# Scattering expert results into token order with an adding transfer, and moving the last expert blocks into the last attention

## The chip, the cores and the metric

The kernel runs on one core of a Trainium2 chip. The metric is the device time of one execution in microseconds (us). Five engines run beside one another, each through its own list of instructions in order: TensorE (PE) multiplies matrices, VectorE (DVE) and ScalarE (ACT) work element by element, GpSimd (POOL) does so too and issues indirect transfers, and SyncE (SP) issues plain transfers. They wait for one another through semaphores. Transfers run on 16 DMA engines that all queues share.

## The reference

There are 8 images of 256 channels and 1024 positions (32 x 32), in float32. Three parts follow one another for each image:

```python
# layer 0: attention with 8 heads of 64, the softmax over the queries
qkv = xt @ w_qkv + b_qkv                       # (8, 1024, 1536)
attn = softmax(einsum('bihd,bjhd->bijh', q, k) * SCALE, axis=1)
x = einsum('bijh,bjhd->bihd', attn, v) @ w_out + b_out + xt
# layer 1, attention over the 1024 tokens of an image
n = ln(t);  t = t + softmax((n @ W.T) @ n.T) @ n
# layer 1, experts: each token goes to the best two of eight
n = ln(t)
combine = weights of the two best of softmax(n @ router_w.T), normalised
out = n
for e in range(8):
    y = gelu(n @ w1[e] + b1[e]) @ w2[e] + b2[e]
    out = out + combine[:, e] * y
t = t + out
```

All sizes of the expert part are 256. The output goes back to channels by positions.

## The kernel before, in words

The main loop at the end of the function goes through the images b = 0 to 7. For each it calls `layer0` (the 8-head attention, in which PE alternates score products and value products), `attend` (the second attention) and `normed` (the norm and the router's logits). While `attend` runs, a function `fill(place)` is called at named places, to put other work into PE's gaps: for images 0 to 6 that is `Begin.at`, which computes the next image's values and its first queries and keys.

Images 0 to 6 form one group of 7168 tokens. For each of them `dispatch` works out, on DVE, a row for every token and each of its two experts, in a DRAM table `rows` that has one stretch of 7168 rows for each expert. Sixteen indirect transfers on POOL (L1081), one for each 128 tokens and choice, write the normed tokens there; they are sent one by one during the next image's `layer0`. The table is filled with zeros at the start (`prepare`, 7 transfers of 8 MB, L295). The token's own sum so far (t2 plus its norm) is kept in DRAM as `sums`, one 1 MB tensor for each image.

When image 7 is in its `layer0`, `plan` counts the tokens of each expert and divides them into 63 blocks of 256 rows, with an address of rows and of weights for each. `experts` then runs the 63 blocks between `layer0` and `attend` of image 7. A block passes through these steps, in different turns of one loop:

- `fetch`: SP loads 256 rows as four transfers (L1252), into one of four buffers; `turned` transposes them on DVE (L1258).
- `hidden`: PE multiplies by the first weight matrix (`ph`, L1269) and ACT applies gelu (`hb`, L1279).
- `collect`: PE multiplies by the second matrix (`pe`, L1295), DVE adds the bias and writes `yb` (L1305, two buffers). POOL issues the gather of the weights for the block four ahead (L1235, which moves nothing if the weights are the same as those in place) and then stores `yb` as rows of a DRAM tensor `y` (L1312).

In the same loop DVE takes one step of `places` for a block, which works out, for each token, where its two results lie in `y`.

`Results` brings the results home. It runs beside `attend` and `dense` of image 7, and a table `PLACES` says at which of their steps how many units are gathered, added and stored. A unit is 128 tokens: two indirect gathers from `y` on POOL (L1391), two multiply-adds on DVE with the gates as factors (L1413), into a tile loaded from `sums`. When an image is whole, `store` transposes each half on DVE (L1449) and sends it out with four transfers of SP.

Image 7 itself has its experts in `dense`: all eight experts on all 1024 tokens, 16 steps of 512 tokens, each with a first product (L1518), a gelu (L1527), a second product (L1542) and four multiply-adds of DVE (L1551).

In `attend` the scores of two blocks of 128 tokens are a `Pair`; `turn` transposes a block of the softmax with DVE and with 16 moves of 32 partitions (L844), half by ACT and half by transfers of SP; `turn_now` does so on PE; `mix` multiplies it by the tokens (`py`, L861). Every engine's instructions run in the order in which the program lists them; `issue_after` and `add_manual_dep` put an instruction behind another.

Of the kernel before, what the change touches and what calls it, by code (L numbers as in the profile page):

```python
# [10 lines left out]
F32 = mybir.dt.float32  # L11
# [8 lines left out]
def kernel(  # L20
# [40 lines left out]
    NXB = NWB + 1  # L61
    SQ = 32
# [3 lines left out]
    WHOLE = 1.5 * 2**23  # L66
# [174 lines left out]

    class Norm:
# [42 lines left out]
    def prepare():  # L285

        zero = wbs[0][:, : 2 * D]
        with tc.issue_after(evicted[0, 0, 1].ins):
            nc.vector.memset(zero, 0.0)

        def fill(group):

            per = E * group.cap // (2 * P)
            return [
                nc.sync.dma_start(  # L295
                    group.rows.rearrange("(p c r) d -> p c (r d)", p=P, r=2)[:, c : c + 32],
                    zero.unsqueeze(1).to_broadcast([P, 32, 2 * D]),
                )
                for c in range(0, per, 32)
            ]  # L300

        first = fill(groups[0])[0]
        with tc.issue_after(first.ins):
            pack()

# [79 lines left out]
    class Begin:  # L385
# [36 lines left out]
        def at(self, place):  # L422

            if place == "norm 1":
                self.project(True)
            elif place == "norm 2":
                with tc.issue_after(evicted["mixed"].ins):
                    self.project(True)
            self.values(1)
# [248 lines left out]
    def attend(b, t1, fill, tick=nothing):  # L678
# [51 lines left out]
        class Pair:  # L730
# [19 lines left out]
            def middle(self, behind=None):  # L750
                far = self.ex[1][:, HALF:]
                with tc.issue_after(behind.ins) if behind else nullcontext():
                    self.product(self.x, s2_, t2_, False)
                self.second = nc.scalar.copy(self.ex[0][:, HALF:], self.x)
# [73 lines left out]
        def turn(i, ex, behind=None):  # L828
# [11 lines left out]
            for a in range(NQ):  # L840
                for k in range(NQ):
                    move = nc.sync.dma_start if (a + k) % 2 else nc.scalar.copy
# [37 lines left out]
        pairs = [Pair(0).middle(), Pair(1).middle()]  # L880
# [6 lines left out]
        pairs[2].middle(evicted["mixed"])  # L887
# [5 lines left out]
        mix(*third)  # L893
        pairs[3].middle()
# [85 lines left out]
    class Group:  # L980


        def __init__(self, n, items):
# [3 lines left out]
            self.rows = dram.tile([E * self.cap, D], F32, name=f"rows_{n}")  # L987
            self.views = dram_disjoint_views(self.rows, 2 * NT * len(items))
            self.y = dram.tile([self.nb * BR, D], F32, name=f"y_{n}")
            self.sums = [dram.tile([P, NT, D], F32, name=f"sums_{b}") for b in items]  # L990
            self.counts = None
            self.kept = {}
# [3 lines left out]
    def normed(b, t2, fill, tick=nothing, norm=None):  # L996

        if norm is None:
            n2 = one.tile([P, NT, D], F32, tag="n", name=f"n2_{b}")
            tick("normed", layer_norm(t2, n2, 1e-5, f"f{b}"))  # L1000
        else:
            n2 = norm.dst
# [3 lines left out]
        tick("turned", to_channels(n2, nT, f"n2_{b}"))  # L1006

        nc.gpsimd.tensor_add(t2, t2, n2)  # L1008
# [4 lines left out]
    def dispatch(b, n2, l, group):  # L1013
# [44 lines left out]
        kept = []  # L1058
        ats = []
        for k in range(2):  # L1060
# [3 lines left out]
            row = keep.tile([P, NT], F32, tag=f"row{k}", name=f"row{k}_{b}")  # L1064
            nc.vector.tensor_reduce(row, sel, AX.X, ALU.add)
            nc.vector.tensor_mul(sel, hot, e_iota.unsqueeze(1).to_broadcast([P, NT, E]))
            exp = keep.tile([P, NT], F32, tag=f"exp{k}", name=f"exp{k}_{b}")
# [3 lines left out]
            kept.append((row, exp))  # L1071
# [3 lines left out]
        group.kept[b] = gate, kept  # L1075

        for k in range(2):
            for i in range(NT):
                behind = yield
                view = group.views[2 * (NT * group.items.index(b) + i) + k]  # L1080
# [9 lines left out]
    def plan(group):  # L1090
# [6 lines left out]
        def tmp(tag, shape, dtype=F32):  # L1097
# [16 lines left out]
        first = keep.tile([P, E], F32, tag="first", name=f"first_{n}", bufs=2)  # L1114
# [5 lines left out]
        turns = keep.tile([P, 1], F32, tag="turns", name=f"turns_{n}", bufs=2)  # L1120
# [17 lines left out]
        nc.vector.tensor_add(block, block, after)  # L1138
        base = tmp("p_base", [E])
        nc.vector.tensor_scalar_mul(base, first, -float(BR))  # L1140
        nc.vector.tensor_scalar(
            first[:, E // 2 :], first[:, E // 2 :], left, None, ALU.subtract
        )
        group.first = first, turns
# [9 lines left out]
        nc.vector.tensor_scalar_min(e_of, e_of, float(E - 1))  # L1154
# [12 lines left out]
        nc.vector.tensor_scalar_min(lo, lo, float(cap - BR))  # L1167
        nc.vector.scalar_tensor_tensor(lo, e_of, float(cap), lo, ALU.mult, ALU.add)
        row_at = keep.tile([P, NBMAX], I32, tag="row_at", name=f"row_at_{n}", bufs=2)
# [14 lines left out]

    def places(group):

        first, turns = group.first
        for b in group.items:
            gate, kept = group.kept[b]
            ats = []  # L1190
            for k, (row, exp) in enumerate(kept):
                hot = small.tile([P, NT, E], F32, tag="d_sel", name=f"p_hot_{b}_{k}", bufs=1)
                nc.vector.tensor_tensor(
                    hot,
                    exp.unsqueeze(2).to_broadcast([P, NT, E]),
                    e_iota.unsqueeze(1).to_broadcast([P, NT, E]),
                    ALU.is_equal,
                )
                nc.vector.tensor_mul(
                    hot, hot, first.unsqueeze(1).to_broadcast([P, NT, E])  # L1200
                )
                to = small.tile([P, NT], F32, tag="d_to", name=f"p_to_{b}_{k}", bufs=2)
                nc.vector.tensor_reduce(to, hot, AX.X, ALU.add)
                nc.vector.scalar_tensor_tensor(to, to, float(BR), row, ALU.mult, ALU.add)
                yield
                pos = small.tile([P, 2, NT], F32, tag="d_pos", name=f"p_pos_{b}_{k}", bufs=2)
                nc.vector.tensor_scalar(
                    pos[:, 0], to, 0.5 - BR / 2, 1.0 / BR, ALU.add, ALU.mult
                )
                nc.vector.tensor_scalar_add(pos[:, 0], pos[:, 0], WHOLE)  # L1210
                nc.vector.tensor_scalar(pos[:, 1], exp, E / 2 - 0.5, None, ALU.is_gt)
                nc.vector.scalar_tensor_tensor(
                    pos[:, 0], pos[:, 0], -WHOLE, pos[:, 1], ALU.add, ALU.add
                )
                nc.vector.tensor_scalar(
                    pos[:, 0], pos[:, 0], turns, float(BR), ALU.min, ALU.mult
                )
                nc.vector.tensor_add(to, to, pos[:, 0])
                at = keep.tile([P, NT], I32, tag=f"yat{k}", name=f"yat{k}_{b}")
                nc.vector.tensor_copy(at, to)  # L1220
                ats.append(at)
                if k > 0:
                    group.kept[b] = gate, ats
                yield

    def experts(group, behind):
# [17 lines left out]
        def fetch(b):  # L1244
            xr = rowp.tile([P, RUN, DQ], F32, tag="xr", name=f"xr_{n}_{b}")
            with tc.issue_after((loads[-1] if loads else evicted["relayed"]).ins):
                at = nc.sync.value_load(
                    row_at[0:1, b : b + 1], min_val=0, max_val=E * group.cap - BR
                )
            mine = group.rows[bass.ds(at, BR), :].rearrange("(s t) (k d) -> k t s d", s=RUN, k=NQ)  # L1250
            for k in range(NQ):
                loads.append(nc.sync.dma_start(xr[ts(k, SQ)], mine[k]))  # L1252
            return xr
# [10 lines left out]
        def hidden(b, xb):  # L1264
# [11 lines left out]
            hT = two.tile([P, NFC, BR], F32, tag=f"qk{b % 2}", name=f"hb_{n}_{b}")  # L1276
# [11 lines left out]
        def collect(b, hT, last, squares):  # L1288
# [3 lines left out]
            with tc.issue_after(last.ins):  # L1292
                for r in range(R):
                    for fc in range(NFC):
                        nc.tensor.matmul(  # L1295
# [8 lines left out]
            with tc.issue_after(squares.ins):  # L1304
                added = nc.vector.tensor_add(  # L1305
# [3 lines left out]
                )  # L1309
            if b + NXB < group.nb:  # L1310
# [341 lines left out]
```

## Time and profile before

| what | value |
|---|---|
| median of 3 runs | 2332.85 us (2331.51 to 2340.35) |
| the profiled execution's own time | 2328.95 us |
| its span, first to last instruction | 2327.1 us |
| PE, DVE, ACT, POOL busy | 97%, 67%, 50%, 18% of the span |
| last `layer0` ends, expert blocks begin | about 1870 us |
| first and last yb add of the expert blocks (L1305) | 1876.1 and 2097.8 us |
| first scores product of the last attention (L708) | 2099.65 us |
| first product of the dense stage (L1518) | 2195.22 us |

A line of the profile names the place in the kernel (L1305), the engine, the operation, the tiles written and read (`yb<-pe,wb`), and, in brackets, how long the engine was idle before it and what ended that. POOL's "busy" for a transfer is the time to issue it; the transfer lands later, which shows only in the wait of an instruction that needs it. "issue" is idle time for which the profile shows no releaser. The median of the runs stands 3.9 us above the profiled execution.

### The profile page before, as it was taken

Reading aid. Unit: us, or ns where it says so; the run is one execution under the profiler, and the core shown is the slowest. Engines: PE = TensorE matmul, PEld = TensorE weight load, DVE = VectorE, ACT = ScalarE, POOL = GpSimd, SP = SyncE. Lnnn points to the kernel's source line nnn. Section 1 sums busy time; section 2 is a strip of 40 time slices with the busy share of each in tenths; the row PEclk is TensorE's granted clock in tenths of the full one; section 3 lists DMA queues with packets and bytes.
Section 4 is the critical chain, followed back from the end, with each engine's and each line's share of the span. In section 5 each row is a group of like instructions: output and inputs, shape, how many; then the busy total and the mean of one; then the engine's idle time right before and its main releaser. Section 6 shows DMA issues by size and latency. Waiting matters only on the chain.

```text
span 2327.1 us, 37989 instructions
## 1 busy us (share of the span) xinstructions
PE 2261.6 (97%) x13059; PEld 1216.1 (52%) x13059; DVE 1554.5 (67%) x4029; ACT 1163.0 (50%) x2138; POOL 410.7 (18%) x392
## 2 busy tenths in 40 slices
PE   9999999999999999999999999999999999998798
PEld 3345533563456335643564355435553488884565
DVE  5775687567855786578657775777568766436655
ACT  3664466456635663656365646465646622225211
POOL 0000012000200020003000200020002135545563
PEclk9999999999999999999999999999999999999899
DMA  8995201020103010201020101100111157765574
GB/s 294 385 386 154 68 17 39 9 56 13 44 2 62 8 49 1 46 19 53 3 46 19 49 8 29 36 26 13 23 42 42 49 145 192 192 199 145 154 210 113
DMA packets 278759, 200.10 MB, mean 86 GB/s; under 512 B 189576, under 2 KB 232232, under 8 KB 276776
## 3 DMA queue, kind: packets, MB, share of 16 engines
q1 hardware_dynamic: 252472, 139.14, 21.2%
q0 software_dynamic: 25008, 58.01, 7.8%
q8 instruction: 104, 1.70, 0.3%
q10 hardware_dynamic: 1088, 0.52, 0.1%
q14 instruction: 87, 0.71, 0.1%
HBM read 108.88 MB, written 110.90 MB: 94 GB/s over the span
## 4 chain that ended last, share of the span: by engine, by line
PE 80%; ACT 5%; DVE 4%; issue 4%; DMA 3%; POOL 3%; SPq 1%; another core or an unknown queue 0%; DVEq 0%; ACTq 0%; POOLq 0%
PE po L569 19%; PE psc L492 19%; PE py L861 7%; PE pqk L371 7%; PE pr L671 5%; PE pv L408 4%; PE ps L761 4%; PE ph L1269 3%; PE pe L1295 3%; PE px L708 2%; POOL yk L1391 2%; PE pqk L349 2%; PE ps1z L761 2%; DMA y<-yb 1%; ACT aT L844 1%
## 5 line engine op out<-in xcount | busy, mean ns | idle before, releaser
L533 ACT ACTIVATE ex<-psc,nmax 128x1024 f32<-128x1024 f32 x512 | 570.0, 1114 | 299.8 <-DVE scrap L516 217.4
L492 PE MATMUL psc<-qk,qk 64*64 64x512 f32 x4096 | 575.8, 593 | 3.8 <-ACT ex L533 3.5
L569 PE MATMUL po<-ex,vs 64*64 64x512 f32 x4096 | 570.6, 591 | 3.6 <-DVE vs L549 2.6
L516 DVE TENSOR_SCALAR_CACHE_REDUCE scrap<-psc,nmax 128x512 f32<-128x512 f32 x512 | 384.2, 750 | 160.3 <-PE psc L492 133.6
L507 DVE TENSOR_REDUCE nmax<-psc 128x1 f32<-128x512 f32 x512 | 350.1, 684 | 9.3 <-PE psc L492 9.3
L492 PEld LDWEIGHTS psc<-qk,qk 64*64 64x64 f32 x4096 | 180.4, 132 | 279.2 <-ACT ex L533 132.6
L569 PEld LDWEIGHTS po<-ex,vs 64*64 64x64 f32 x4096 | 176.5, 132 | 275.6 <-DVE vs L549 82.1
L1081 POOL DMA_INDIRECT rows<-n,d_at x112 | 109.0, 973 | 661.1 <-DVE nmax L507 660.8
L1008 POOL TENSOR_TENSOR t<-t,n 128x2048 f32<-128x2048 f32 x8 | 36.3, 4535 | 875.5 <-DVE n L263 875.5
L371 PE MATMUL pqk<-xT,wqkv 128*128 128x512 f32 x384 | 171.2, 599 | 0.0
L861 PE MATMUL py<-n,spare 128*128 128x256 f32 x512 | 122.0, 394 | 11.3 <-DMA out_dram<-oT 3.8
L336 ACT ACTIVATE qk<-pqk,b_qks 128x512 f32<-128x512 f32 x124 | 85.6, 690 | 86.7 <-PE pqk L371 77.6
L1391 POOL DMA_INDIRECT yk<-y,yat x112 | 111.3, 994 | 76.4 <-issue 28.4
L371 PEld LDWEIGHTS pqk<-xT,wqkv 128*128 128x128 f32 x384 | 71.0, 190 | 99.9 <-issue 77.0
L408 PE MATMUL pv<-wqkv,xT 128*128 128x512 f32 x256 | 121.5, 599 | 1.5 <-DVE v L416 1.0
L861 PEld LDWEIGHTS py<-n,spare 128*128 128x128 f32 x512 | 100.7, 198 | 38.1 <-issue 23.9
L671 PE MATMUL pr<-wo,res 128*128 128x256 f32 x512 | 111.9, 379 | 0.7 <-ACT res L588 0.7
L844 ACT COPY spare<-home 32x256 f32<-32x256 f32 x256 | 103.0, 402 | 10.0 <-DVE home L833 6.7
L671 PEld LDWEIGHTS pr<-wo,res 128*128 128x128 f32 x512 | 97.2, 190 | 17.7 <-ACT res L588 4.7
L1279 ACT ACTIVATE hb<-ph,wb 128x256 f32<-128x256 f32 x96 | 40.1, 470 | 126.9 <-issue 89.4
L533 ACT ACTIVATION_READ_ACCUMULATOR ex<-psc,nmax 128x1 f32 x512 | 99.1, 194 | 0.0
L870 DVE SCALAR_TENSOR_TENSOR t<-py,rs,t 128x256 f32<-128x256 f32 x64 | 30.5, 476 | 98.0 <-PE py L861 85.3
(256 smaller groups left out, 2939.7 us busy)
## 6 DMA issues: line engine op xcount, KB each, us to landing
rows<-wb SPq DMA_DIRECT2D x7, 8192.0 KB
xr<-rows SPq DMA_DIRECT2D x252, 64.0 KB
y<-yb POOLq DMA_DIRECT2D x63, 256.0 KB
xs<-in_x_dram SPq DMA_DIRECT2D x64, 128.0 KB
spare<-home SPq DMA_DIRECT2D x256, 32.0 KB
out_dram<-oT SPq DMA_DIRECT2D x60, 128.0 KB
xT<-in_x_dram SPq DMA_DIRECT2D x7, 1024.0 KB
sums<-t SPq DMA_DIRECT2D x7, 1024.0 KB
```

The costliest lines, as they stand in the source:

```text
L371: mm = nc.tensor.matmul(pq[:, ts(n, 512)], wqkv[:, cc, t, ts(g, P)], xT[:, cc, ts(n, 512)], start=(cc == 0), stop=(cc == NCC - 1),)
L408: nc.tensor.matmul(pv, self.xT[:, cc, ts(i, P)], wqkv[:, cc, 2, :], start=(cc == 0), stop=(cc == NCC - 1),)
L492: mm = nc.tensor.matmul(pss[at, h][ts(c, DK), ts(n, 512)], k[r, j * P + c * DK : j * P + (c + 1) * DK], q[r, ts(n, 512)], start=True, stop ...
L507: firsts[at, h] = nc.vector.tensor_reduce(nmax, pss[at, h][:, ts(0, 512)], AX.X, ALU.max, negate=True)
L516: seconds[h] = nc.vector.tensor_scalar(scrap, pss[at, h][:, ts(1, 512)], -1.0, nmaxes[at, h], ALU.mult, ALU.min, accum_out=nmax,)
L533: nc.scalar.activation(ex, pss.pop((at, h)), AF.Exp, bias=nmaxes.pop((at, h)), scale=1.0, accum_out=sums[at][:, h : h + 1],)
L569: mm = nc.tensor.matmul(po[n][ts(h, DK), :], vss[at][keys, h, :], exps[at, h][keys, ts(n, 512)], start=(j == 0 and turn == 0), stop=(j == ...
L671: nc.tensor.matmul(pr[:, :C], res[:, g, ts(i, P)], wo[:, g, :], start=(g == 0), stop=(g == NPAIR - 1))
L761: return nc.tensor.matmul(to, stationary[:, ts(self.k, P)], moving, start=start, stop=True, skip_group_check=not start,)
L844: move(to[ts(k, SQ), a], since[ts(a, SQ), k])
L861: evicted["mixed"] = nc.tensor.matmul(py[:, :D], aT[m], n1[:, m, :], start=(m == 0), stop=(m == NT - 1))
L1391: ins = nc.gpsimd.indirect_dma_start(out=self.slot(at)[:, k, :], out_offset=None, in_=self.group.y[:, :], in_offset=bass.IndirectOffsetOnAxis(
```

## The change

It has three parts.

1. *Rows carry gate and destination.* A row of `rows` has 258 numbers instead of 256: the token, its gate, and a number that gives its place in `sums`. POOL writes the two columns (a copy and an iota) before each group of eight row scatters. `sums` becomes one tensor of 14336 rows in token order, twice: the first half begins as each image's own sum, the second half as zeros (`clear`, one 7 MB transfer of SP ahead of image 1). In `experts`, a fifth load a block brings gate and place (`where`); DVE multiplies `yb` by the gate and works out the place; and two indirect transfers on POOL with an addition in the transfer (128 rows of 1 KB each) add `yb` to `sums`. Rows that no token fills have a place out of bounds and are skipped. `places`, the tensor `y` and its plain store are gone.
2. *`Results`* now loads both halves of an image's sums, 1 MB each, with plain transfers of POOL, adds them with DVE in halves of an image, one at each step of `dense`, and stores them a step later. It begins behind the norm, so nothing of it is left in the last attention.
3. *The last four blocks* (`LATE`) finish inside image 7's attention: their second products at the places "between", "between 2" and "norm 2", and the first products of the last two at "last weights". For this `Pair.middle` is split in two, in all images, one value block of `Begin.at` moves from "last products" to "between", and block 6's `turn` uses two transfers fewer and two ACT copies more. The dense stage's second and third weights are loaded behind the norm instead of ahead of it.

```diff
+    DW = D + 2
 class Group:
-            self.rows = dram.tile([E * self.cap, D], F32, name=f"rows_{n}")
+            self.rows = dram.tile([E * self.cap + BR, DW], F32, name=f"rows_{n}")
-            self.y = dram.tile([self.nb * BR, D], F32, name=f"y_{n}")
-            self.sums = [dram.tile([P, NT, D], F32, name=f"sums_{b}") for b in items]
+            self.sums = dram.tile([2 * self.cap, D], F32, name=f"sums_{n}")
+            self.ways = dram_disjoint_views(self.sums, R * self.nb)
+    def clear(group):
+        pieces = group.sums[group.cap :].rearrange("(p c r) d -> p c (r d)", p=P, r=2)
+        nc.sync.dma_start(
+            pieces,
+            wbs[0][:, : 2 * D].unsqueeze(1).to_broadcast([P, group.cap // (2 * P), 2 * D]),
+        )
 def dispatch:
+                if i == 0:
+                    nc.gpsimd.tensor_copy(n2[:, :, D], gate[:, k, :])
+                    nc.gpsimd.iota(
+                        n2[:, :, D + 1],
+                        [[-1, NT]],
+                        base=2 * group.cap - (k * len(group.items) + which) * S,
+                        channel_multiplier=-NT,
...
 def experts, fetch:
+            where = small.tile([P, R, 2], F32, tag="where", name=f"where_{n}_{b}", bufs=8)
+            loads.append(
+                nc.sync.dma_start(
+                    where, group.rows[bass.ds(at, BR), D:].rearrange("(r p) c -> p r c", r=R)
+                )
+            )
 def experts, collect:
             yb = two.tile([P, R, D], F32, tag="yb", name=f"yb_{n}_{b}")
...
+                where = wheres.pop(b)
+                nc.vector.tensor_mul(yb, yb, where[:, :, 0:1].to_broadcast([P, R, D]))
+                to = small.tile([P, R], I32, tag="to", name=f"to_{n}_{b}", bufs=4)
+                nc.vector.tensor_scalar(
+                    to, where[:, :, 1], -1.0, float(2 * group.cap), ALU.mult, ALU.add
+                )
             if b + NXB < group.nb:
                 weights(b + NXB)
-            nc.gpsimd.dma_start(group.y[ts(b, BR), :].rearrange("(r p) d -> p r d", r=R), yb)
-            if b >= NXB:
-                with tc.issue_after(added.ins):
-                    next(placed, None)
+            for r in range(R):
+                nc.gpsimd.indirect_dma_start(
+                    out=group.ways[R * b + r][:, :],
+                    out_offset=bass.IndirectOffsetOnAxis(ap=to[:, r : r + 1], axis=0),
+                    in_=yb[:, r, :],
+                    in_offset=None,
+                    bounds_check=2 * group.cap - 1,
+                    oob_is_err=False,
+                    compute_op=ALU.add,
+                )
+            return mm
 experts, the loop:
-            if b - 3 in rows:
+            if b - 3 in rows and b - 3 < group.nb - LATE // 2:
-            if b - 4 in hiddens:
+            if b - 4 in hiddens and b - 4 < group.nb - LATE:
 Results:
+            nc.gpsimd.dma_start(self.totals[n], self.group.part(0, n))
+            nc.gpsimd.dma_start(self.seconds[n], self.group.part(1, n))
+            n, h = self.todo.pop(0)
+            some = self.totals[n][:, ts(h, NB), :]
+            with tc.issue_after(behind.ins):
+                nc.vector.tensor_add(some, some, self.seconds[n][:, ts(h, NB), :])
 turn:
-                    move = nc.sync.dma_start if (a + k) % 2 else nc.scalar.copy
+                    away = (a + k) % 2 and (i < 6 or a > 0)
+                    move = nc.sync.dma_start if away else nc.scalar.copy
 the main loop, image 7:
-        experts(groups[0], evicted["divided"])
-        others = Results(groups[0])
-        others.begin()
+        product, result = experts(groups[0], evicted["divided"])
...
+            if place == "between":
+                result(end - 4)
+            elif place == "between 2":
+                result(end - 3)
+            elif place == "last weights":
+                product(end - 2)
+                product(end - 1)
+            elif place == "norm 2":
+                with tc.issue_after(evicted["mixed"].ins):
+                    result(end - 2)
+                    result(end - 1)
```

## The prediction

> **What bounds the kernel now.** I read the page's chain first. It is PE for 80% of the span, and through the first seven images PE is never idle, so nothing that merely frees another engine gains there. The change works on the end, from the expert blocks (about 1870 us) on, so I asked for busy time by stretch: the last image's attention, the same stretch of image 6 (which has no expert results to add), and the expert blocks. The columns are stretch, length, busy time of PE, PEld, DVE, ACT, POOL with instruction counts, granted clock, DMA share, GB/s.
>
> ```profile
> 2099.60:2183.90 84.30, 70.49 (x216) 43.61 (x216) 53.42 (x121) 40.62 (x89) 49.76 (x50) 0.90 0.64 170
> 1634.20:1702.10 67.90, 65.17 (x225) 40.36 (x224) 35.76 (x85) 40.41 (x89) 0.00 (x0) 1.00 0.24 39
> 1878.00:2084.00 206.00, 200.78 (x921) 173.46 (x919) 101.88 (x268) 48.62 (x116) 103.96 (x116) 1.00 0.68 187
> ```
>
> The last attention takes 16.4 us longer than image 6's, with 17.7 us more DVE work: the result adds and output transposes. The expert blocks are PE-bound (97%), but not by much. In the timeline there (start, duration, instruction, idle time before it with its releaser) I followed one yb buffer round:
>
> ```profile
> 1968.42 0.69 DVE L1305 TENSOR_TENSOR yb<-pe,wb 128x512 f32<-128x512 f32 x1 [0.89 <-PE pe L1295]
> 1969.86 1.03 POOL L1235 DMA_INDIRECT wb<-wpack,w_at  x1 [1.66 <-issue]
> 1970.88 0.77 POOL L1312 DMA_DIRECT2D y<-yb  x1
> 1976.22 0.69 DVE L1305 TENSOR_TENSOR yb<-pe,wb 128x512 f32<-128x512 f32 x1 [1.78 <-DMA y<-yb]
> ```
>
> The add fills yb at 1968.42; POOL starts the next weight gather 1.44 us later, then the store; the buffer is free for the next-but-one block when the store has landed, 4.57 us after its issue ended. One turn is 7.80 us. There are two yb buffers, so a turn over 6.90 us (two PE blocks of 3.45) eats slack. The yb tile's own table (us, times) shows that it often does:
>
> ```profile
>   DVE yb L1305: 45.1, 20
> ```
>
> PE keeps its pace only because these waits are occasional. From the first yb add (1876.1) to that of block 58 (2084.82) the mean is 208.7/58 = 3.60 us a block. Last, POOL when its indirect transfers follow one another:
>
> ```profile
> 2208.44 0.95 POOL L1391 DMA_INDIRECT yk<-y,yat  x1 [0.30 <-issue]
> 2209.70 0.99 POOL L1391 DMA_INDIRECT yk<-y,yat  x1 [0.30 <-issue]
> 2210.99 0.95 POOL L1391 DMA_INDIRECT yk<-y,yat  x1 [0.30 <-issue]
> 2212.25 0.95 POOL L1391 DMA_INDIRECT yk<-y,yat  x1 [0.30 <-issue]
> ```
>
> Each starts about 1.26 us after the one before: 0.95 busy and 0.30 of issue. The direct store above followed its gather with no such gap.
>
> **What the Trainium skill says.** "DMA: Bandwidth & Descriptors", Anatomy of one DMA (SWDGE path): most of the fixed cost of a POOL transfer is waiting for the write's receipt, and HBM is the slowest target. The trace agrees: stores land 3.66 to 6.3 us after their issue ends. The same page, Rules for kernel authors: an accumulating DMA reads its destination and writes it later. No accumulating DMA is in this trace. "Collectives: The Full Stack", The bandwidth ceiling: an add in the DMA engine costs a second source read and about halves the rate; not shown here either. "Perfetto Trace Analysis", GPSIMD Engine Instruction: POOL durations are to be taken from start-to-start spacing, which is why I use 1.26 and not 0.95.
>
> **The change, part by part.** *Expert loop.* Out go the small DVE operations that worked out row addresses (0.16 to 0.23 us each, some 11 for two blocks, on a DVE busy 49%): no gain. The one store of a block becomes two indirect scatters with addition; DVE gets a second pass over yb (taken as the add's 0.69, waiting for the add) and one small operation (0.17); SP gets a fifth load a block (8-byte pieces; one issue more at a median of 0.32 us, on a queue that loads up to four blocks ahead, so hidden). In the built program POOL's order is weights, scatter, scatter for each block, and the add of block b waits for both scatters of block b-2. So the turn is: 1.44 to the weight gather, 1.33 to the first scatter (1.03 and 0.30; yb is ready by then, at about 1.44 + 0.3), 1.26 to the second, 0.97 for it (the mean of the row scatters in the page), then L, the landing: 5.00 + L. While DVE waits for it, the transposes of later rows and the adds are queued behind, and PE's next product waits for the accumulator that the add would free. The pace is then half a turn.
>
> L is not in this trace. Lower end: 3.66, the last stores, with little other traffic (issued 2093.40 + 0.72, buffer written at 2097.78). Upper end: 6.26, a store during a weight load (2038.71 + 0.76 to 2045.73). The second scatter has half the bytes but is read and written and has the first just ahead of it; I take 4.8, a little above the loaded 4.57. A gain on L below 3.66 isn't excluded for half the bytes, nor a cost above 6.26 for the addition; both are rivals below.
>
> The turn is 9.8, the pace 4.9. Block 58 is the last whose result is taken in the loop: 1876.1 + 58 x 4.9 = 2160.3, and with 1.5 us for its second pass the attention's first copy (nT) starts at 2161.8. Before, it started at 2098.38, after all 63 blocks. The change is +63.4 us here. That already credits the loop with the products that move out of it (four second products and two first ones, 6 x 1.73 = 10.4 us).
>
> *Last attention.* Image 6 took 67.90. Take out its two value blocks (2 x 1.72), put in two first and two second expert products (4 x 1.73): 71.4, say 72, against 84.3: -12.3. Two more second products fall in the norm, where PE idled 3.48 us. There DVE loses 3.8 us of adds and transposes and gains 2.8 us of expert results: -1.
>
> *Dense stage.* 112 gathers and 112 DVE adds (479 ns) become 14 loads of 1 MB and 14 half-image adds (some 1.25 us each, taken from the 128x1024 transposes). PE lost 3.7 us in 2260 to 2300 behind the gathers: -4. The first load waits for the last scatters, which stand behind the 4.5 us POOL add: about 4.5 + 4 x 1.26 + 4.8 + 7 for 2 MB = 21 us after the norm, some 4 us past its first use, of which PE's other work covers half: +2. Sum -2.
>
> *Hidden parts.* The gate and destination columns and their iotas are on POOL, idle in image 6's attention and nearly so elsewhere. The 7 MB clear goes once on SP, 19 us of DMA at 390 GB/s, beside image 1's PE-bound layer; SP's first zero fill issued in 0.4 us and the next took 21.5, so it is hidden unless a queue entry behind it has to wait for room: then up to 19 us. The reordering of value blocks in the other attentions shifts PE work; image 6 idles 2.7 us, so 0 with at most a few us either way for all seven.
>
> *Sum.* 63.4 - 12.3 - 1 - 2 = +48.1. The profiled execution took 2328.95 (span 2327.1), so 2377 of that kind; the median of the runs is 3.9 above it: 2332.85 + 48.1 = 2381.
>
> **The rivals.** With the tail worth -15.3, the turn decides: the change breaks even when 58 paces = 2098.38 - 1877.6 + 15.3 = 236.1, a pace of 4.07, L = 3.14.
> *B, POOL's issue is the bound.* Three indirect starts a block are 1.33 + 1.26 + 1.26 = 3.85, already over PE's 3.45. If scatters land within 2.7 us it sets the pace: 223.3 - 236.1 = -13, 2320. For it: half the bytes; against: 3.66 for an almost undisturbed store.
> *C, the turn stays hidden and the change is faster.* If the 0.30 gaps overlap and the landing is short, the pace stays at 3.60: 208.8 - 236.1 = -27, 2306 (at 3.45, 2297). Its place is the yb wait; it decides from a turn of 7.2 us down. For it: the tail gain is clear in the profile. Against: the turn is 7.8 today with one transfer.
> *D, the addition is slow.* If a scatter with addition takes L = 8, the pace is 6.5: 377 - 236.1 = +141, 2474. For it: the second read; against: the DMA engines are 68% busy and a block's scatters double only 23% of that (POOL's queue took 35.0% of 16 engines for 25.02 MB in 224 us: 50 ns a KB, so 256 KB over 16 engines is 0.8 of 3.45 us).
> *E, the clear or the reordered attentions stall the front,* the turn as forecast: up to +19, 2400.
>
> **How the numbers follow.** Forecast (L 3.66 to 6.26, so 2348 to 2423; its own range) 0.52, B 0.13, C 0.15, D 0.15, E 0.05. A measurement here can tell about 0.5% (11.7 us) from no change. Faster: C and over half of B, 0.23. Same (2321 to 2345): the rest of B and the forecast's lower edge, 0.09. Slower 0.68. The range reaches from the middle of C, 2304, to the start of D, 2440, leaving out 0.08 and 0.12.
>
> **What would show it.** Right: DVE's yb add idle for most of each block behind the scatters' landing; yb adds of one buffer 9 to 11 us apart; PE about 70% busy in the expert stage; attention 70 to 75 us. Wrong: PE still 95% busy there (C), POOL busy with 0.3 gaps and no DVE wait (B), or turns above 12 us (D).

## The result: 87 us slower, and the profile after

| | before | after |
|---|---|---|
| median (range) | 2332.18 us (2328.99 to 2340.35, 4 runs) | 2419.43 us (2418.46 to 2421.18, 4 runs) |
| span of the profiled execution | 2327.1 us | 2417.9 us |

The ratio is 1.0369, with an interval of 1.0342 to 1.0397. Cut the two profiled executions at the same three events (the first yb add; px, the last attention's first product; and the end of its last product, py), and the 90.8 us between the spans have a place:

| stretch | before | after | difference | forecast |
|---|---|---|---|---|
| start to the first yb add | 1876.1 | 1903.2 | +27.1 | 0 |
| first yb add to px | 223.6 | 308.7 | +85.1 | +63.4 |
| last attention, px to the end of py | 84.2 | 69.4 | -14.8 | -12.3 |
| norm and dense stage, to the end | 143.2 | 136.6 | -6.6 | -3 |

Busy time by stretch of the changed kernel, with the columns of the prediction's table (length; PE, PEld, DVE, ACT, POOL; clock, DMA share, GB/s): the last attention and the expert loop.

```profile
2211.90:2281.30 69.40, 68.75 (x249) 45.03 (x250) 39.36 (x94) 44.38 (x97) 10.85 (x8) 1.00 0.33 58
1903.00:2209.00 306.00, 230.76 (x942) 185.19 (x943) 119.11 (x234) 48.92 (x117) 250.41 (x173) 0.95 0.77 123
```

The attention is full of PE work. In the loop PE has sunk to 75% and POOL has risen to 250.41 busy. POOL issued 173 transfers there, and the timeline shows 0.30 us ahead of each: 250.4 + 173 x 0.30 = 302 of 306 us. POOL's queue is full. One block's turn, in the timeline of the changed kernel (DVE and POOL lines):

```profile
1992.15 0.69 DVE L1324 TENSOR_TENSOR yb<-pe,wb 128x512 f32<-128x512 f32 x1 [3.51 <-DMA sums<-yb,to]
...
1995.31 1.07 POOL L1246 DMA_INDIRECT wb<-wpack,w_at  x1 [0.30 <-ACT hb L1298]
1996.68 1.58 POOL L1338 DMA_INDIRECT sums<-yb,to  x1 [0.30 <-issue]
...
1998.57 1.96 POOL L1338 DMA_INDIRECT sums<-yb,to  x1 [0.31 <-issue]
...
2000.83 1.07 POOL L1246 DMA_INDIRECT wb<-wpack,w_at  x1 [0.30 <-issue]
...
2003.35 0.69 DVE L1324 TENSOR_TENSOR yb<-pe,wb_x 128x512 f32<-128x512 f32 x1 [3.64 <-DMA sums<-yb,to]
```

The block added at 1992.15 has its scatters issued only from 1996.68 on, because POOL is still at the block before and then at the next gather. From there: 1.58, 0.31 and 1.96 us of issue, and the buffer is free at 2003.35, only 2.82 us after the second issue ended. The page has the two kinds of scatter side by side, that with addition and the plain one of the rows, both of 128 rows of about 1 KB:

```profile
L1338 POOL DMA_INDIRECT sums<-yb,to x126 | 206.9, 1642 | 78.9 <-DVE yb L1330 41.3
L1132 POOL DMA_INDIRECT rows<-n,d_at x112 | 109.1, 974 | 515.5 <-DVE nmax L527 476.8
```

One with addition takes 1.64 us of POOL, a plain one 0.97 (means). So a block asks POOL for 1.07 + 1.64 + 1.64 + 3 x 0.30 = 5.25 us, and the first 59 yb adds came at (2209.2 - 1903.2)/58 = 5.28. The yb tile's own table names another wait:

```profile
  DVE yb L1324: 168.9, 52
```

That is what the prediction had said to look for. It is also what a full POOL queue looks like from DVE: a buffer whose scatters were issued late comes free late. The experiments had to tell the two apart.

DMA by queue in the same loop, before and after (packets, MB, share of 16 engines):

```profile
q0 software_dynamic: 13312, 25.02, 35.0%
```

```profile
q0 software_dynamic: 24768, 22.36, 48.7%
```

POOL's queue took 35.0% of 16 x 224 us for 25.02 MB before, 50 ns a KB (1000 bytes); after, 48.7% of 16 x 306 us for 22.36 MB, 107 ns a KB. The weights in it move as before, so the adding part costs at least twice what a plain one does in DMA time. That agrees in direction with what "Collectives: The Full Stack", The bandwidth ceiling, says of an add in the DMA engine (a second source read).

### The profile page after: what moved, and what is told of

Read it like the earlier page. It is cut to its first block, busy times and chain, and to the rows that moved or that the text cites. A ratio compares the mean times of both kernels' runs of the same rounds, so it can differ in the third digit from the quotient of the medians.

```text
span 2417.9 us, 38077 instructions
## 1 busy us (share of the span) xinstructions
PE 2281.0 (94%) x13059; PEld 1221.9 (51%) x13059; DVE 1553.8 (64%) x3904; ACT 1172.8 (49%) x2156; POOL 469.7 (19%) x386
## 4 chain that ended last, share of the span: by engine, by line
PE 66%; SPq 11%; DMA 6%; DVE 6%; issue 5%; ACT 5%; POOL 1%; DVEq 0%; POOLq 0%; ACTq 0%
PE po L589 16%; PE psc L512 16%; PE py L885 7%; SPq L306 7%; PE pqk L390 6%; PE pr L691 4%; PE ps L784 3%; PE pv L427 3%; PE pdy L1522 2%; PE px L728 2%; SPq L1263 2%; PE pqk L368 2%; PE pdh L1498 2%; DMA sums<-yb,to 2%; DMA where<-rows 2%
## 5 line engine op out<-in xcount | busy, mean ns | idle before, releaser
L1338 POOL DMA_INDIRECT sums<-yb,to x126 | 206.9, 1642 | 78.9 <-DVE yb L1330 41.3
L1287 PE MATMUL ph<-xb,wb 128*128 128x256 f32 x384 | 104.8, 420 | 60.4 <-DVE xb L1276 41.0
L1324 DVE TENSOR_TENSOR yb<-pe,wb 128x512 f32<-128x512 f32 x48 | 33.1, 690 | 141.0 <-DMA sums<-yb,to 123.5
L885 PE MATMUL py<-n,spare 128*128 128x256 f32 x512 | 116.5, 380 | 4.4 <-DMA spare<-home 2.1
L1287 PEld LDWEIGHTS ph<-xb,wb 128*128 128x128 f32 x384 | 75.9, 206 | 86.3 <-DVE xb L1276 55.5
L868 ACT COPY spare<-home 32x256 f32<-32x256 f32 x272 | 109.4, 402 | 11.8 <-DVE home L856 8.1
```

Of the source, the lines that this page charges most:

```text
L885: evicted["mixed"] = nc.tensor.matmul(py[:, :D], aT[m], n1[:, m, :], start=(m == 0), stop=(m == NT - 1))
L1287: last = nc.tensor.matmul(ph[:, ts(fc, BR)], wb[:, dc * FF + fc * P : dc * FF + (fc + 1) * P], xb[:, dc, :], start=(dc == 0), stop=(dc == ...
L1338: nc.gpsimd.indirect_dma_start(out=group.ways[R * b + r][:, :], out_offset=bass.IndirectOffsetOnAxis(ap=to[:, r : r + 1], axis=0), in_=yb[ ...
```

## The experiments

The runs were made in several sets, and the kernel before had medians from 2317 to 2335 us in them, so a difference of 15 us between medians of two sets is not read. The verdicts rest on one stretch of each kernel's profile, from the first yb add to px, and on one window inside the loop, 1910 to 2130 us. DVE has four instructions a block there, so its count gives the pace (for the kernel before, the prediction's mean of 58 blocks stands in the column). The stretch holds all 63 blocks of the kernel before and of the one without late blocks, and 59 of the others. Three kernels whose loop is that of the changed one (changed, zero fill, and the first attempt at more work on POOL) have stretches of 308.7, 311.5 and 311.7 us, so a few us there say nothing.

| kernel | median us | ratio to before | first yb add to px, us | us a block, from DVE's count |
|---|---|---|---|---|
| before | 2332.2 | 1 | 223.6 | 3.60 |
| changed | 2419.4 | 1.0369 | 308.7 | 5.21 (169) |
| plain scatters | 2388.7 | 1.0263 | 281.8 | 4.68 (188) |
| third yb buffer | 2415.1 | 1.0376 | 304.9 | 5.09 (173) |
| zero fill in 2048-byte pieces | 2408.4 | 1.0339 | 311.5 | 5.30 (166) |
| no load of gate and place | 2420.3 | 1.0398 | 314.3 | 5.37 (164) |
| plain, third yb buffer | 2394.9 | 1.0252 | 283.1 | 4.78 (184) |
| no weight gathers | 2342.9 | 1.0031 | 230.0 | 3.89 (226) |
| gathers that move nothing | 2419.6 | 1.0442 | 313.4 | 5.30 (166) |
| plain, gathers that move nothing | 2345.9 | 1.0124 | 235.1 | 3.98 (221) |
| more work on POOL | 2479.9 | 1.0702 | 369.4 | 6.29 (140) |
| three plain regions | 2383.2 | 1.0205 | 281.6 | 4.68 (188) |
| no late blocks | 2450.9 | 1.0584 | 329.3 | 5.18 (170) |

**Plain scatters.**

```diff
                     oob_is_err=False,
-                    compute_op=ALU.add,
```

> The scatters write plainly instead of adding; this leaves out the addition, so the sums of a token's first choice lose its own value. Theory 1 (POOL's issue of the adding scatters is the bound: 1.07 + 1.58 + 1.58 to 1.98 and three gaps of 0.30 make 5.1 to 5.5 us a block): a plain scatter issues in 0.97, so POOL needs 1.07 + 0.97 + 0.97 + 0.90 = 3.9 us a block, the loop shortens by 58 x (5.28 - 3.9) = 80 us, about 2340 us. Theory 2 (the landing of the addition in the DMA engines is the bound, the issue only reflects it): POOL's issue stays near 1.58 or the wait for the landing grows, and less than 30 us are gained.

The median was 2388.72 us, ratio 1.0263 (1.0242 to 1.0283). By the ratios that is 25 us less, and the stretch is 26.9 us shorter. The size is the second theory's (less than 30 us). What that theory rests on is not seen: the issue did not stay near 1.58. POOL in the timeline of this kernel, where it runs freely:

```profile
1993.92 1.05 POOL L1246 DMA_INDIRECT wb_x<-wpack,w_at  x1 [0.30 <-issue]
1995.27 1.00 POOL L1338 DMA_INDIRECT sums<-yb,to  x1 [0.30 <-issue]
1996.58 1.07 POOL L1338 DMA_INDIRECT sums<-yb,to  x1 [0.31 <-issue]
1997.96 1.04 POOL L1246 DMA_INDIRECT wb<-wpack,w_at  x1 [0.30 <-issue]
```

Without the addition a scatter takes 1.0 us, and a block 4.04. From the first scatter's start to the second's it is 1.31 us, with addition 1.89. But the mean was 4.7 us a block: something else held the loop in places. The next runs look for the first bound and for this second one.

**A third yb buffer.**

```diff
+    ybp = ctx.enter_context(tc.tile_pool(name="ybp", bufs=3))
-            yb = two.tile([P, R, D], F32, tag="yb", name=f"yb_{n}_{b}")
+            yb = ybp.tile([P, R, D], F32, tag="yb", name=f"yb_{n}_{b}")
```

> Three yb buffers instead of two, nothing else. The recorded forecast (half a turn of two yb buffers sets the pace): a third buffer makes the pace a third of the turn of 10.5 us, below PE's 3.45, so the loop falls to POOL's or PE's floor; if that were 3.9 as in the recorded sum, -75 us, about 2345. Theory 1 (POOL is busy all the time, 250 of 306 us plus 173 gaps of 0.30): DVE's wait moves to another place and the time stays within 5 us of 2419.

The median was 2415.11 us, ratio 1.0376 (1.0355 to 1.0397), and the stretch 3.8 us shorter. The wait for a yb buffer fell from 168.9 to 96.0 us:

```profile
  DVE yb L1325: 96.0, 30
```

That made the loop hardly faster, so the number of buffers, and with it the forecast's half turn, is not the bound.

**Zero fill in 2048-byte pieces.** The table is filled as one flat stretch, in aligned pieces of 2048 bytes, not in pieces of two rows (2064).

```diff
-            pieces = group.rows.rearrange("(p c r) d -> p c (r d)", p=P, r=2)
+            flat = group.rows.rearrange("a d -> (a d)")
...
+            pieces = flat[: per * P * 512].rearrange("(p c w) -> p c w", p=P, w=512)
...
```

> The zero fill of the row table is written in aligned pieces of 2048 bytes over the flat table instead of pieces of 2064 bytes; the same bytes are zeroed. Theory F (the longer and slower fill, which ends some 14 us later, holds back the 64 moves of image 0's attention on SP): the second image's output products begin about 411 to 412 us instead of 426.8 and the time falls by 14 to 16 us, to about 2404. Theory C (the 7 MB clear on SP, or the reordered attentions, hold the front back): no change, 2417 to 2421.

The median was 2408.35 us, ratio 1.0339 (1.0322 to 1.0357). All DMA from 30 to 150 us, nearly all of it the fill, in the kernels before, after, and with 2048-byte pieces:

```profile
DMA packets 22600, 46.25 MB, mean 385 GB/s; under 512 B 80, under 2 KB 80, under 8 KB 22589
```

```profile
DMA packets 20841, 42.98 MB, mean 358 GB/s; under 512 B 79, under 2 KB 79, under 8 KB 20830
```

```profile
DMA packets 22599, 46.24 MB, mean 385 GB/s; under 512 B 80, under 2 KB 80, under 8 KB 22588
```

The fill does stall the front. What stands behind it on SP are image 0's moves for `turn` (aT): they went at 212.12 us before, at 231.59 after, and here at 220.53. In the changed kernel PE waited for them:

```profile
238.74 5.90 PE L885 MATMUL py<-n,aT 128*128 128x256 f32 x16 [7.46 <-DMA aT<-home]
```

Image 1's output products (pr) then began 15.8 us later than before (426.81 against 410.96); here at 415.10, 11.7 us earlier than in the changed kernel. The span is 10.3 us shorter, though the intervals of the two ratios overlap. Other profiles bear the front out: in nine whose front is that of the changed kernel this moment lies between 424.2 and 436.1, and in the second kernel with the new fill (three plain regions, below) it is 413.00. The remaining 4.1 us may lie with further entries on SP's queue (eight entries of the fill took 147.32 us there and a ninth followed; before there were seven, in 125.07); that was not tried. "DMA: Bandwidth & Descriptors", How a descriptor splits into AXI transactions, says that a descriptor that does not start on 256 bytes fetches bytes that it does not use. Most pieces of 2064 bytes start so in the table, but there they are written, of which the page says nothing, and size and alignment were changed together here. So no run shows which it was.

**No load of gate and place.**

```diff
-            where = small.tile([P, R, 2], F32, tag="where", ...)
-            loads.append(nc.sync.dma_start(where, ...))
+            where = fixed
```

> The fifth load of a block is left out; gate 1 and a fixed place for each row stand in its stead, so the sums are other ones, with the same number of scatters and adds (only the last blocks' rows are skipped, instead of the empty rows). Theory 3 (the 8-byte pieces of that load hold up the row loads and so PE): the pace falls from 5.28 by 0.4 or more, -25 us or more. Theory 1: within 8 us of 2419, since POOL does the same work.

The median was 2420.31 us, ratio 1.0398, the stretch 5.6 us longer: no gain. The fifth load of a block was hidden, as forecast. Some 3.7 of the 5.6 us are an earlier start of the stretch: the first yb add comes 20.0 us after image 7's first output product here, as in the kernel before, and 23.7 us after it in the changed kernel.

**Plain scatters with a third buffer.** The two edits above together.

> Leaves out the addition (plain scatters) and adds a third yb buffer. In the run with plain scatters alone a block took 4.7 us in the expert loop: GpSimd's work was down to 1.05 + 1.00 + 1.00 us and three gaps of 0.30, 3.95 in all, but the yb adds still waited 53.5 us for scatters, 0.9 us per block. Theory 1 (GpSimd's issues come first, the turn of a buffer second): with both removed the loop runs at 3.95 per block, 58 x (4.7 - 3.95) = 44 us less, about 2345 us. Theory 2 (the transfers of rows and weights hold the loop once the issues are short): the third buffer gives less than 10 us, 2380 to 2390.

2394.91 us, ratio 1.0252 (1.0230 to 1.0275), the stretch 1.3 us longer than with plain scatters alone. The buffers are not the second bound either, and the first theory, which had a buffer's turn come next, falls.

**No weight gathers after the first four.**

```diff
-            if b + NXB < group.nb:
-                weights(b + NXB)
```

> Leaves out every gather of weights after the first four, so most blocks are computed with another expert's weights; the adding scatters stay. Theory 1 (the loop waits for GpSimd's issues): a block is rid of 1.07 + 0.30 us on GpSimd, 58 x 1.37 = 79 us, about 2340 us. Theory 2 (the landing of the adding scatters holds a yb buffer): only the wait of the scatters behind a gather goes, less than 30 us, 2390 to 2420.

2342.92 us, ratio 1.0031 (1.0022 to 1.0040): 77 us less, and the stretch 78.7 us shorter, as the first theory had said. Busy time from 1910 to 2130 us, this kernel:

```profile
1910.00:2130.00 220.00, 208.83 (x908) 170.34 (x907) 114.77 (x226) 47.84 (x114) 174.27 (x112) 0.99 0.89 130
```

PE is back at 95%, with both adding scatters still in place and the DMA engines at 89%. So neither the scatters' landing nor the DMA engines' load as such forces 5.28 us a block. The pace is 3.89, not the 3.60 of before. POOL's queue has a little room now (174.27 + 112 x 0.30 = 207.9 of 220 us); a yb buffer's turn, 7.50 us in one place (from 1981.71 to 1989.21), is close to two blocks. Which of the two holds the loop at 3.89 was not tried. And the edit removes two things, a place in POOL's queue and a transfer.

**Gathers that move nothing.** All gathers stay in the queue; those after the first four get an index out of bounds.

```diff
-        nc.vector.scalar_tensor_tensor(
-            hi[:, NXB:], same[:, NXB:], float(E * P), hi[:, NXB:], ALU.mult, ALU.add
-        )
+        nc.vector.tensor_scalar_add(hi[:, NXB:], hi[:, NXB:], float(E * P))
```

> Keeps every gather of weights in GpSimd's queue but gives all of them after the first four an index out of bounds, so that nothing is moved (most blocks then use another expert's weights). It splits what leaving the gathers out altogether gave, 77 us: the place in the queue (1.07 + 0.30 us per block) from the transfer (up to 650 KB, when a block's expert is new to its buffer). Theory 1 (GpSimd's queue is the bound): the period stays 1.07 + 1.58 + 1.58 to 2.0 + 3 x 0.30 us, at least 5.1 per block, 2405 to 2420 us. Theory 2 (the weights' transfer delays what is behind it in the same DMA queue, and the scatters' landing with it): most of the 77 us goes, 2340 to 2370.

2419.58 us, ratio 1.0442 (1.0411 to 1.0472), the stretch 4.7 us longer: nothing gained. The same window:

```profile
1910.00:2130.00 220.00, 165.05 (x672) 131.40 (x671) 84.58 (x166) 35.20 (x84) 182.40 (x124) 0.95 0.70 96
```

The DMA share fell to 70% and the pace stayed. So the transfer alone was worth nothing, and the gain of the run before needed the 1.37 us of queue to go. Whether their going would have given all of it with the transfers still there, no run shows. The first bound is settled from one side. Nor is an adding scatter's issue long because the DMA engines are busy: its mean in this window is 1.69 us at a DMA share of 70%, 1.65 in the changed kernel at 77%, and 1.56 without gathers at 89%.

**More work on POOL.** The first attempt added two additions of 128x256 behind each block's scatters, with nothing in the block that they depended on.

```diff
+            for _ in range(2):
+                nc.gpsimd.tensor_add(spin, spin, spin)
```

> Two more additions of 128x256 on GpSimd behind each block's scatters, which nothing reads. The same addition took 0.72 us elsewhere in the profile of the changed kernel. Theory 1 (GpSimd's queue is the bound of the loop): 58 x 1.45 = 84 us more, about 2503 us. Theory 2 (landings or the DMA engines are the bound, GpSimd has time left): less than 30 us more, 2420 to 2450.

2451.87 us, ratio 1.0493, 32 us more. It says nothing of the loop: the additions all ran at the start of the kernel, from 6.1 to 92.6 us (the first yb add came at 1934.1, 31 us later), and the stretch from there to px was 311.7 us, as in the changed kernel. Tied to their block they stay where they should:

```diff
+                nc.gpsimd.tensor_add(spin, spin, where[:, :, 0:1].to_broadcast([P, R, P]))
```

> Two more additions of 128x256 on GpSimd for every block, which nothing reads. In the earlier run they depended on nothing in their block and were all placed ahead of the loop; here each reads its block's gates, so that they stay between the scatters. The same addition took 0.72 us elsewhere in the profile. Theory 1 (GpSimd's queue is the bound of the loop): 58 x 1.45 = 84 us more than the changed kernel, about 2503 us, 2480 at the least. Theory 2 (landings or DMA engines are the bound): less than 30 us more, 2420 to 2450.

2479.93 us, ratio 1.0702 (1.0671 to 1.0733). POOL in the timeline of this kernel:

```profile
1995.33 1.08 POOL L1246 DMA_INDIRECT wb<-wpack,w_at  x1 [0.22 <-issue]
1996.71 1.57 POOL L1338 DMA_INDIRECT sums<-yb,to  x1 [0.30 <-issue]
1998.59 1.55 POOL L1338 DMA_INDIRECT sums<-yb,to  x1 [0.31 <-issue]
1999.60 1.87 POOL L1348 TENSOR_TENSOR spin<-spin,where 128x256 f32<-128x256 f32 x2
2001.69 1.08 POOL L1246 DMA_INDIRECT wb_x<-wpack,w_at  x1 [0.22 <-issue]
```

From gather to gather it is 6.36 us, 1.08 more than 5.28, and 58 x 1.08 = 63; the stretch grew by 60.7. The expected 84 was wrong because a block paid only 1.08 for 1.87 of additions: they overlap the end of the scatter before them in the record (start 1999.60, that scatter's end 2000.14), and the second scatter lost its excess over 1.58. POOL has no gap in that turn but those of issue, so what its queue got longer by, the loop got slower by. With the gathers that move nothing, this shows POOL's queue as the bound from both sides.

**Plain scatters, gathers that move nothing.** The two edits together, for the second bound.

> Leaves out the addition (plain scatters) and the transfer of weights after the first four blocks; every instruction of GpSimd stays. With plain scatters alone a block took 4.7 us where GpSimd's issues ask for 3.95, and a third yb buffer gave nothing. Theory 3 (the rest of the loss is the weights' transfers: the waits come where an expert is new to a buffer): the loop reaches GpSimd's 3.95 or PE's pace, 58 x 0.75 = 44 us less than with plain scatters alone, about 2345 us. Theory 4 (the row loads and their place on SP hold the loop): less than 10 us, 2380 to 2390.

2345.89 us, ratio 1.0124 (1.0094 to 1.0153), the stretch 46.7 us shorter than with plain scatters alone, 3.98 us a block: POOL's own sum. These are waits from 1910 to 2130 us in the kernel with plain scatters alone (engine, line, waited for: us, times, longest; "remote" is a releaser that the profile can't name):

```profile
DVE yb L1324 <- DMA sums<-yb,to: 38.9, 15, 4.0
DVE yb L1324 <- remote: 31.4, 6, 5.8
...
POOL wb L1246 <- ACT hb L1298: 25.5, 10, 3.1
PE ph L1287 <- DVE xb L1276: 21.8, 10, 3.8
```

With gathers that move nothing the second is gone, the third is 0.3 us and the fourth 16.3. The first has risen to 100.2 us, although the loop is faster: POOL's queue is full again, and the wait for a buffer shows it. So behind the addition lay a second bound, weights' transfers that are no longer hidden. It costs 47 us when the first is lifted and nothing while POOL is slower. Why the kernel before hid the same transfers is open. There POOL was idle half the time, so a gather went out as soon as its buffer was free, not behind two scatters; that is argued, not shown.

**Three plain regions.** Token sums, first and second choice each have a region of their own. The scatters are plain, nothing is cleared, and `Results` loads three regions and adds twice; a third yb buffer and the 2048-byte fill are in.

```diff
-            self.sums = dram.tile([2 * self.cap, D], F32, name=f"sums_{n}")
+            self.sums = dram.tile([3 * self.cap, D], F32, name=f"sums_{n}")
...
-            clear(groups[0])
...
-                    compute_op=ALU.add,
...
+            for _ in range(2):
                 if self.todo:
                     self.add(behind)
```

> Plain scatters into two regions that only they write, beside the token sums in a third; the last stage loads all three and adds twice, so nothing is left out and nothing need be cleared. With a third yb buffer and the zero fill in 2048-byte pieces. Theory 1: like plain scatters with a third buffer (2345 expected) less 11 us for the fill, if the further 7 loads of 1 MB and 14 additions of 1.2 us (17 us of VectorE's 142 us in the last stage) stay hidden: about 2335 us, close to the kernel before. Theory 2: as there, 2370 to 2380.

2383.19 us, ratio 1.0205 (1.0180 to 1.0229). By the ratios that is 1.6% faster than the changed kernel and still 2% slower than before: its loop has the pace of plain scatters alone, 4.68 us a block, so the second bound is presumably in it too. No version here beats the kernel before. The norm and dense stage took 140.0 us against 136.6, so the further loads and adds may not have been quite hidden.

**No late blocks.** All 63 blocks in the loop, none in the last attention.

```diff
-    LATE = 4
+    LATE = 0
```

> The changed kernel with all 63 blocks in the expert loop and none inside the last attention; nothing is left out. It prices the third part of the change. Theory A (the four blocks cost the attention only their PE time): the loop takes 4 x 5.28 = 21 us more, the attention, whose PE was busy 71.45 of 72.1 us, is rid of 4 x 3.6 = 14 us of PE work and takes about 58 us: 7 us slower than the changed kernel, 2426 us. Theory B (the attention has a chain of its own that lasts about 72 us, the blocks ran in its gaps for nothing): 21 us slower, 2440 us. Theory C (the blocks hinder the attention): no slower, 2415 us or less.

2450.93 us, ratio 1.0584 (1.0567 to 1.0602). The stretch to px is 20.6 us longer, which is 4 x 5.15, and the attention is no shorter: 73.2 us from px to the end of py, against 69.4. (The first yb add was 7.1 us later too, in a part that the edit doesn't touch; with the attention that makes the 11 us by which the median stands above theory B's.) Theory B stands: the four blocks cost the attention nothing.

## Why the prediction was right, and where not

It said slower and 2381 us; 2419 is inside the range of 2304 to 2440 and inside the forecast's own 2348 to 2423. The sign and the place are right: the expert loop got slower, by far more than the tail gained. The mechanism is not the forecast's, and two terms of the sum failed.

- **The bound of the loop.** The step that failed is "the pace is then half a turn", with L = 4.8. The landing measured 2.4 to 2.8 us in the turns of that timeline, below the lower end of 3.66. With 2.82, and the issues as priced, the turn would have been 7.8 us, 3.9 a block. What sets the pace instead is the sum of POOL's queue, 5.25 us a block, and the wrong price in it is the term "1.26 to the second, 0.97 for it": the issue of an adding scatter, taken from plain ones, is 1.64 us. With that the turn is 9.2 us. The rest of the measured 10.6 (2 x 5.28) is time that the block stands in the full queue: the next gather starts 3.16 us after the yb add in the timeline above, not 1.44. So rival B's queue was 5.25 a block and not 3.85, above the forecast's 4.9. B had the mechanism and the wrong price; it was given 2320 us and a chance of 0.13. That the forecast came near is luck: two errors of opposite sign, a landing 2.0 us too long and issues too short, and 58 x (5.28 - 4.9) = 22 us are its remaining miss. The unknown price was bounded for the landing alone; the issue of an adding scatter, which stood in no trace either, got no range.
- **The signs to look for.** yb adds of one buffer 9 to 11 us apart (10.6), PE about 70% busy (75%), DVE idle behind landings: all came true, under another cause. B's sign, "POOL busy with 0.3 gaps and no DVE wait", left out that a full queue makes the same DVE wait.
- **Addition in the DMA engines (D).** Its time did double, but it doesn't set the pace: without the gathers the loop ran at 3.89 us a block with a DMA share of 89%. There, and with plain scatters and gathers that move nothing, POOL's queue moves little but the scatters (1903 to 2180 and 1910 to 2180 us):

```profile
q0 software_dynamic: 17280, 14.54, 42.8%
```

```profile
q0 software_dynamic: 13973, 14.31, 17.6%
```

  That is 130 ns a KB with addition and 53 without. Part of the difference may be that the DMA engines were fuller in the first.
- **Last attention.** -12.3 forecast, -14.8 measured. In the run without late blocks it is 11.0 us shorter than before, so the gain is the work that left it, and the four blocks cost it nothing.
- **Norm and dense.** -3 forecast, -6.6 measured. PE is busy 125.8 us in both kernels; it idled 17.4 us before and 10.9 after. The idle time that went is 6.5 us, where the forecast's dense stage had counted on 3.7. (The stage now holds two expert blocks' second products as well; the mean clock was 0.96 against 0.93.)
- **Hidden parts.** The clear was hidden: it was issued in 0.60 us at 270 us, and the kernel with three plain regions, which has no clear, begins image 1's output products only 2.1 us earlier than the one with the same fill. The front was not 0, but +27.1 us, beyond rival E's +19 too. The step that failed is the list under *Hidden parts*, which has no entry for the fill, although its rows had grown from 1024 to 1032 bytes. It cost 15.8 us by image 1 in this profile. From there the delay grew to 23.3 us at image 7's output products, about 1.3 us an image, where the reordered blocks and the writes of gate and place are; which of them it was, was not tried. The last 3.7 us are ACT's order of work: DVE waited 4.43 us for `rstd_a` before the first yb add (0.27 before), because ACT had two blocks' gelus ahead of it. In the run without the load of gate and place `rstd_a` comes first again, and the 3.7 us are gone.

## What to carry to other kernels

An engine that issues indirect transfers is a resource with a sum of its own. Add up issue times and gaps for each turn of a loop, and bound the price of any kind of issue that the trace doesn't show, as one does for a landing. A wait for a buffer doesn't tell whether the transfer was slow or issued late; here it rose from 38.9 to 100.2 us in an edit that made the loop faster. To find out, keep the instruction and take away what it moves, or put more work in the queue, tied to the loop by data so that it stays there.

## What was not expected of the hardware

- An indirect scatter of 128 rows of 1 KB took POOL 1.54 to 2.09 us with addition (median 1.58) and 0.97 to 1.41 without (median 1.00), to the same table by the same indices.
- An indirect gather all of whose indices are out of bounds still took 1.07 us of POOL.
- Adding scatters of 128 KB landed 2.4 to 2.8 us after their issue ended, sooner than the plain 256 KB store of the kernel before (4.57).
- Zero pieces of 2064 bytes were written at 358 GB/s, pieces of 2048 at 385.
